# First attention of a two-layer decoder: the order of three engines, the sums of queries, and who normalizes

## The chip, the cores and the metric

The kernel runs on one core of a Trainium2 chip. A core has five engines that run side by side and meet only through semaphores: TensorE (PE, matrix products and transposes, result in PSUM), VectorE (DVE), ScalarE (ACT), GpSimd (POOL, which cannot read PSUM) and SyncE (SP, which here only issues DMAs). The metric is device microseconds of one execution; the median of several runs is compared.

## The reference, cut to what matters

A batch of 16 sequences of 112 tokens with 256 features passes through two decoder layers (attention, cross attention, mixture of experts, each behind a layer norm and with a residual). The change is in the first attention, a linear attention with 16 heads of 16 features:

```python
q = jax.nn.softmax(to_heads(q), axis=-1); k = jax.nn.softmax(to_heads(k), axis=-1)
comp_q = 1.0 - q; comp_k = 1.0 - k
def feat(x): return jnp.concatenate([x * sin, x * cos], axis=-1)
def branch(qf_, kf_):
    kv = jnp.einsum('bhld,bhlm->bhdm', kf_, v)
    z = 1.0 / jnp.maximum(jnp.einsum('bhld,bhd->bhl', qf_, kf_.sum(axis=2)), EPS)
    return jnp.einsum('bhld,bhdm,bhl->bhlm', qf_, kv, z)
attn = branch(qf, kf) + branch(comp_qf, comp_kf)
```

`sin` and `cos` depend on the token alone. The softmax of a query is its exponentials over their sum; the kernel works with the exponentials and puts the sums in at the end.

## The kernel before, in words

The whole program is one function, unrolled. A planner orders the instructions of each engine by a simulation of its own; inside `tc.manual_schedule(engines=...)` the engines named run their instructions in the order of the code. Before, the first attention names PE alone, so DVE, POOL, ACT and SP follow the planner. Each engine executes its queue strictly in order: an instruction that waits holds up all that stand behind it.

x stays in SBUF for the whole kernel (`x_res`). Its first two batches are loaded on SP, then Wq, Wk and Wv, then two more batches, then three groups of four, then Wo. ACT's queue loads the early constants, the output biases `bo2` of two attentions and the projection biases.

The stage is a software pipeline over the batches. Iteration i of its loop (L497) calls, for different batches:

- `norm0(i+2)` (L376): statistics on DVE (L232, L233), variance to a reciprocal root on POOL (L240, L241), normalization on DVE (L236), and the output bias added to x on POOL (L383).
- `norm0_T(i+1)` (L386): two transposes on PE, a copy on ACT (L390).
- `project0(i)` (L392): q, k and v products on PE (their matmuls all carry L115), biases added on DVE (L399, L403), the maximum of each head (L401), its subtraction on POOL (L404), exponentials on ACT (L405).
- `features(i-1)` (L408): q times sine and cosine on ACT (L415), transposes (L420), copy (L422); on DVE the sums of the exponentials of q and k (L425), reciprocals of the latter (L427), times sine and cosine (`rs`, L429); v scaled by them, one half on DVE and one on POOL (L433), with `rs` as eight more columns (L431); the products k by v on PE (L442), masked to the blocks of the heads on DVE (L449).
- `branches(i-2)` (L454): q by the masked product (L115, L458) and a constant product of the values for the complement (L459); the two normalizers z on DVE (L464 to L467), their combinations `sh` (L469, L470), two products into `a` (L472, L478), added on POOL (L484).
- `out_T0(i-3)` (L487): two transposes of `a` (L491), copied on ACT (L492).

In PE's order out_T0(i-3) stands ahead of features(i-1) and branches(i-2). After iteration 8 the vectors of later stages are transposed (`turn_vectors`) and an empty tile is written on POOL and spread to DRAM (`empty_rows`, L343). After the loop 16 output projections are added to x on DVE (L522); the second attention follows, whose own block names PE alone.

Of the kernel before, what the change touches and what calls it, by code (L numbers as in the profile page):

```python
# [33 lines left out]
def _constants():  # L34
# [9 lines left out]
    comp[:L] = both  # L44
    total = np.zeros((128, 1))
    total[:L, 0] = both.sum(axis=0)
    half = np.arange(8)
# [8 lines left out]
        "comp": comp,  # L56
        "total": total,
        "none_id": 2 * NT + p[:, None],
# [35 lines left out]
def tile_decoder(ctx: ExitStack, tc: tile.TileContext, t: dict, out: bass.AP):  # L94
# [38 lines left out]
    bo2 = cp.tile([L, 2, D], F32, tag="bo2", name="bo2")  # L133
    for i, n in enumerate(("L0_attn_bo", "L0_xattn_b_O")):
        nc.scalar.dma_start(bo2[:, i, :], t[n].partition_broadcast(L))

# [30 lines left out]

    w_attn0 = load_w(2 * WR, [t[f"L0_attn_W{n}"] for n in "qkv"])
    load_x(2, 2)
    for g in range(1, 4):  # L170
        load_x(4 * g, 4)
    w_attn0 += load_w(2 * WR + 1536, [t["L0_attn_Wo"]])
    nc.sync.dma_start(call[:, early:], t["consts"][:, early:])


    bV = cp.tile([KC, D], F32, tag="bV", name="bV")
    nc.sync.dma_start(bV, t["L0_xattn_b_V"].partition_broadcast(KC))
# [185 lines left out]
    with ExitStack() as ph:  # L363
# [9 lines left out]
        heads = lambda a: a.rearrange("p (f h) -> p f h", f=2)  # L373
        qks, vas, tots, qfs, kvs, outs = {}, {}, {}, {}, {}, {}

        def norm0(b):  # L376
            mv = sm.tile([L, 2], F32, tag="nmv", name="nmv", bufs=4)
            r = sm.tile([L, 1], F32, tag="nr", name="nr", bufs=4)
            xn = lp.tile([L, D], F32, tag="xn", name="xn", bufs=3)
            stats_of(mv, x[:, b, :])  # L380
            rstd_pow(r, mv[:, 1:2])
            normed(xn, x[:, b, :], mv[:, 0:1], r)
            nc.gpsimd.tensor_add(x[:, b, :], x[:, b, :], bo2[:, 0, :])  # L383
            return xn

        def norm0_T(b, xn):  # L386
            pt = bank()
            for c in range(2):
                nc.tensor.transpose(pt[:, c * L : (c + 1) * L], xn[:, c * 128 : (c + 1) * 128], ident[:L, :L])
            nc.scalar.copy(xnT[:, :, b * L : (b + 1) * L], pt[:, : 2 * L].rearrange("p (c l) -> p c l", l=L))  # L390
# [16 lines left out]

        def features(b):  # L408
            qk, va = qks.pop(b), vas[b]
            q = qk[:, :16, :].rearrange("p h d -> p (h d)")  # L410
            k = qk[:, 16:, :].rearrange("p h d -> p (h d)")

            qs = lp.tile([L, 2, D], F32, tag="qs", name="qs")
            for s in range(2):
                nc.scalar.activation(qs[:, s, :], q, AF.Copy, scale=tok[:, s : s + 1])  # L415
            pq = bank()
            for f in range(2):
                for s in range(2):
                    o = (2 * f + s) * L
                    nc.tensor.transpose(pq[:, o : o + L], qs[:, s, f * 128 : (f + 1) * 128], ident[:L, :L])  # L420
            qf = lp.tile([128, 4, L], F32, tag="qf", name="qf")
            nc.scalar.copy(qf.rearrange("p n l -> p (n l)"), pq[:, : 4 * L])  # L422

            tot = sm.tile([L, 32], F32, tag="a0tot", name="tot", bufs=4)
            nc.vector.tensor_reduce(tot, qk, AX.X, ALU.add)  # L425
            rk = sm.tile([L, 16], F32, tag="a0rk", name="rk", bufs=2)
            nc.vector.reciprocal(rk, tot[:, 16:])  # L427
            rs = sm.tile([L, 2, 16], F32, tag="a0rs", name="rs", bufs=2)
            nc.vector.tensor_tensor(rs, bcast(tok, 16), over(rk, 2), ALU.mult)  # L429
            v2 = lp.tile([L, 2, 2, 136], F32, tag="v2", name="v2")  # L430
            nc.gpsimd.tensor_copy(v2[:, :, :, 128:], rs.rearrange("p s (f h) -> p f s h", f=2))  # L431
            for s, e in enumerate((nc.vector, nc.gpsimd)):
                e.tensor_tensor(  # L433
                    v2[:, :, s, :128].rearrange("p f (h m) -> p f h m", m=16),
                    va.rearrange("p (f h m) -> p f h m", f=2, m=16),
                    bcast(heads(rs[:, s, :]), 16),
                    ALU.mult,
                )
            kv = lp.tile([128, 2, 2, 136], F32, tag="kv", name="kv")
            for f in range(2):  # L440
                pk = bank()
                mm(  # L442
                    pk[:, :272],
                    k[:, f * 128 : (f + 1) * 128],
                    v2[:, f].rearrange("p s n -> p (s n)"),
                    start=True,
                    stop=True,
                )
                nc.vector.tensor_tensor(  # L449
                    kv[:, f], pk[:, :272].rearrange("p (s n) -> p s n", s=2), over(block, 2), ALU.mult  # L450
                )
            tots[b], qfs[b], kvs[b] = tot, qf, kv

        def branches(b):  # L454
            qf, kv, tot, va = qfs.pop(b), kvs.pop(b), tots.pop(b), vas.pop(b)
            po, pc = bank(), bank()
            for f in range(2):
                mm_sum(po[:L, f * 136 : (f + 1) * 136], [(qf[:, 2 * f + s, :], kv[:, f, s, :]) for s in range(2)])  # L458
            mm(pc[:L, :D], const("comp", L), va, start=True, stop=True)  # L459
            o3 = po[:L, :272].rearrange("p (f n) -> p f n", n=136)  # L460
            z = sm.tile([L, 2, 16], F32, tag="z", name="z")
            zs = [heads(z[:, i, :]) for i in range(2)]
            sq, zt = heads(tot[:, :16]), o3[:, :, 128:]
            nc.vector.scalar_tensor_tensor(zs[0], sq, EPS_Z, zt, ALU.mult, ALU.max)  # L464
            nc.vector.scalar_tensor_tensor(zs[1], sq, const("total", L), zt, ALU.mult, ALU.add)
            nc.vector.scalar_tensor_tensor(zs[1], sq, EPS_Z, zs[1], ALU.mult, ALU.max)
            nc.vector.reciprocal(z, z)  # L467
            sh = sm.tile([L, 2, 16], F32, tag="sh", name="sh")
            nc.vector.tensor_add(sh[:, 0, :], z[:, 0, :], z[:, 1, :])  # L469
            nc.vector.tensor_mul(sh[:, 1, :], tot[:, :16], z[:, 1, :])  # L470
            a = lp.tile([L, 2, D], F32, tag="a", name="a")
# [21 lines left out]

        with tc.manual_schedule(engines={mybir.EngineType.PE}):
            xns = {b: norm0(b) for b in range(2)}
            norm0_T(0, xns.pop(0))
            for i in range(B + 3):  # L497
                if i < B:
                    project0(i)
                if i + 2 < B:  # L500
                    xns[i + 2] = norm0(i + 2)
                if i + 1 < B:
                    norm0_T(i + 1, xns.pop(i + 1))
                if 0 <= i - 3:
                    out_T0(i - 3)
                if 0 <= i - 1 < B:
                    features(i - 1)
                if 0 <= i - 2 < B:
                    branches(i - 2)
                if i == 8:  # L510
# [960 lines left out]
```

## Time and profile before

| what | us |
|---|---|
| median of 4 runs | 1876.49 (1873.29 to 1878.6) |
| the profiled execution | 1870.06 |
| its span in the profile | 1868.3 |
| PE, DVE, ACT, POOL busy in the span | 1630.1, 969.2, 603.1, 520.6 |
| first projection product of the first attention starts | 16.70 |
| last projection of the first attention starts | 117.58 |
| its output projection starts | 140.55 |

A profile has one row for each instruction or group: line of the kernel, engine, operation, `out<-in` by the names of the tiles, partitions x elements, count, busy time and mean time of one, and the idle time of the engine just before, with what ended it. Windows give each engine's busy time in a stretch. Busy time of PE is of pipelined matmuls, so a busy PE need not be at its peak. A float32 matmul appears as two passes.

### The profile page before, as it was taken

The numbers are of one execution on the slowest core, as the hardware profiler recorded it, in microseconds if no ns is written. First come the engines' busy times: TensorE is split into PE (matmuls) and PEld (weight loads), VectorE is DVE, ScalarE is ACT, GpSimd is POOL, SyncE is SP. The second block draws the span as 40 slices with busy tenths as digits, with TensorE's granted clock in tenths as the row PEclk, the third lists the DMA queues.
The fourth block names the chain that finished last, engine by engine and source line by source line (L and its number), as shares of the span: only waits on it lengthen the run. The fifth ranks groups of instructions, "written<-read, shape, count | busy, mean of one in ns | idle before, by whom it ended". The sixth has DMA issues, their size and how long they took to land. (4 is left out here: it accounts for less than half of the span.)

```text
span 1868.3 us, 31175 instructions
## 1 busy us (share of the span) xinstructions
PE 1630.1 (87%) x11755; PEld 1225.0 (66%) x11755; DVE 969.2 (52%) x2637; ACT 603.1 (32%) x1440; POOL 520.6 (28%) x699
## 2 busy tenths in 40 slices
PE   5877888888992496999999899999998899989992
PEld 4765566666661374778787566666666788878882
DVE  6864566666653243877776544655455532222222
ACT  2430333333340252223323333434432233323330
POOL 5532111111103452333333344444443000030003
PEclk9997999999996698999999999999998899999996
DMA  9401111111102345100000100000001244454422
GB/s 266 139 1 41 41 40 41 42 42 38 40 23 82 111 145 193 50 1 1 1 1 1 40 10 17 18 17 17 17 9 46 74 145 145 152 172 165 158 85 65
DMA packets 93342, 125.60 MB, mean 67 GB/s; under 512 B 17761, under 2 KB 76298, under 8 KB 93194
## 3 DMA queue, kind: packets, MB, share of 16 engines
q1 hardware_dynamic: 85178, 107.88, 18.7%
q0 software_dynamic: 5184, 13.13, 2.3%
q10 hardware_dynamic: 2832, 2.60, 0.5%
q8 instruction: 95, 1.56, 0.4%
q14 instruction: 53, 0.43, 0.1%
HBM read 94.40 MB, written 21.18 MB: 62 GB/s over the span
## 5 line engine op out<-in xcount | busy, mean ns | idle before, releaser
L1193 POOL TENSOR_SCALAR pr<-pr,den 112x375 f32<-112x375 f32 x128 | 156.5, 1241 | 198.3 <-DVE den L1191 192.4
L1373 DVE SCALAR_TENSOR_TENSOR hT<-pT,vT,gt 128x264 f32<-128x264 f32 x128 | 62.9, 492 | 239.6 <-ACT gt L1372 239.4
L115 PE MATMUL pT<-xnT,w_all 128*128 128x224 f32 (+2 forms) x736 | 165.0, 376 | 6.2 <-DVE xnT L267 6.2
L115 PEld LDWEIGHTS pT<-xnT,w_all 128*128 128x128 f32 x736 | 133.8, 198 | 25.8 <-issue 14.6
L641 ACT ACTIVATE pr<-pT 125x336 f32<-125x336 f32 x256 | 94.6, 456 | 164.8 <-PE pT L632 164.8
L1410 POOL DMA_INDIRECT got<-eo,row x32 | 30.1, 941 | 387.2 <-PE pT L115 215.8
L115 PE MATMUL pT<-cT,w_all 128*128 128x375 f32 x384 | 136.8, 497 | 0.2 <-ACT cT L1142 0.2
L616 DVE TENSOR_REDUCE mx<-pT 112x1 f32<-112x375 f32 x256 | 125.7, 539 | 20.7 <-PE pT L614 20.2
L115 PE MATMUL pT<-w_all,cT 128*125 128x256 f32 (+1 forms) x384 | 135.2, 496 | 0.0
L115 PE MATMUL pT<-hT,w_all 128*128 128x264 f32 x512 | 119.6, 393 | 6.3 <-ACT hT L1378 6.3
L115 PE MATMUL pT<-w_all 128*128 128x264 f32 x512 | 119.4, 389 | 0.0
L115 PE MATMUL pT<-e1T,w_all 128*128 128x264 f32 x512 | 116.7, 386 | 0.0
L115 PEld LDWEIGHTS pT<-hT,w_all 128*128 128x128 f32 x512 | 99.1, 194 | 24.2 <-ACT hT L1378 6.7
L1090 POOL TENSOR_TENSOR pr<-pr,den 112x448 f32<-112x448 f32 x64 | 59.3, 948 | 199.1 <-DVE den L1088 142.2
L115 PEld LDWEIGHTS pT<-w_all 128*128 128x128 f32 x512 | 97.4, 192 | 16.4
L115 PEld LDWEIGHTS pT<-cT,w_all 128*128 128x128 f32 x384 | 72.8, 195 | 53.0 <-issue 13.7
L115 PEld LDWEIGHTS pT<-e1T,w_all 128*128 128x128 f32 x512 | 96.7, 190 | 16.1
L115 PE MATMUL pT<-w_all,oT 128*112 128x256 f32 x448 | 106.9, 385 | 0.0
L115 PE MATMUL pT<-w_all,xnT 128*112 128x256 f32 (+1 forms) x320 | 105.2, 477 | 0.9 <-ACT xnT L390 0.9
L115 PEld LDWEIGHTS pT<-w_all,cT 128*125 128x125 f32 x384 | 71.0, 191 | 45.1 <-issue 31.4
L1372 ACT ACTIVATE gt<-pT,vT 128x264 f32<-128x264 f32 x128 | 61.3, 480 | 110.7 <-PE pT L115 89.6
L1182 ACT ACTIVATE pr<-pT,top 112x375 f32<-112x375 f32 x128 | 72.4, 572 | 52.2 <-DVE top L1181 50.2
(247 smaller groups left out, 3018.1 us busy)
## 6 DMA issues: line engine op xcount, KB each, us to landing
w_all<-in_L_ffn_w_c_fc_dram SPq DMA_DIRECT2D x16, 1024.0 KB
w_all<-in_L_ffn_w_gate_dram SPq DMA_DIRECT2D x16, 1024.0 KB
w_all<-in_L_ffn_w_c_proj_dram SPq DMA_DIRECT2D x16, 1024.0 KB
cx<-in_ctx_dram SPq DMA_DIRECT2D x32, 375.0 KB
kz<-kn SPq DMA_DIRECT2D x256, 23.4 KB
xg<-fill SPq DMA_DIRECT2D x1, 5547.0 KB
xb<-xg SPq DMA_DIRECT2D x43, 129.0 KB
eo<-os SPq DMA_DIRECT2D x16, 264.0 KB
```

What stands on the lines that cost most here:

```text
L115: mm(o, l, r, start=(i == 0), stop=(i == len(terms) - 1))
L616: nc.vector.tensor_reduce(mx[b % 2][:, g, i, 16:17], ps[i][:L, :S], AX.X, ALU.max, negate=True)
L641: nc.scalar.activation(pr[:, i, :], pw[i][:KC, : NKC * L], AF.Exp)
L1090: nc.gpsimd.tensor_tensor(pr[:, k], pr[:, k], bcast(den[:, k, :], L), ALU.mult)
L1182: nc.scalar.activation(pr[:, i, :], ps[i][:L, :S], AF.Exp, bias=top[:, i : i + 1], scale=1.0, accum_out=den[:, i : i + 1],)
L1193: nc.gpsimd.tensor_scalar(pr[:, n, :], pr[:, n, :], den[:, n : n + 1], None, ALU.mult)
L1372: nc.scalar.activation(gt, ps[1][:, :HS], AF.Identity, bias=vec(n_v + e * NJ + j), scale=1.0)
L1373: nc.vector.scalar_tensor_tensor(hT[:, j, :], ps[0][:, :HS], vec(12 + e * NJ + j), gt, ALU.add, ALU.mult)
L1410: nc.gpsimd.indirect_dma_start(out=got[:, :], out_offset=None, in_=eo[b // HB][:, :], in_offset=bass.IndirectOffsetOnAxis(ap=row[k][:, b : ...
```

## The change

It does the following, all in the first attention or in the loads ahead of it:

1. PE, DVE and POOL run in the order of the code; the code of the loop is put in a new order. An iteration is now by_place(i-1), project0(i), norm0_T(i+1), features(i-1), norm0(i+2), branches(i-2), out_T0(i-3), stats0(i+3).
2. `norm0` is split: `stats0` makes the statistics and the reciprocal root one iteration earlier; the normalization itself goes from DVE to POOL.
3. `by_place`, new, takes the scaling of q, k and v out of `features`. The copy of `rs` into the eight columns goes from POOL to ACT.
4. The sums of the exponentials of q are no longer reduced on DVE. The tile kv gets eight more columns per half, which hold the block mask; it becomes two fixed tiles whose mask columns are written once. The product with q then yields, beside 136 columns, eight columns with the sum of q times sine plus the sum of q times cosine; ACT scales them by one over (sine + cosine) of the token into `sq`.
5. The clamp of the second normalizer (L466) is dropped.
6. Loads: x of batches 2 and 3 ahead of Wv and not behind it; the bias `L0_xattn_b_O` goes from ACT's queue to a later place in SP's.

```diff
-    w_attn0 = load_w(2 * WR, [t[f"L0_attn_W{n}"] for n in "qkv"])
+    w_attn0 = load_w(2 * WR, [t[f"L0_attn_W{n}"] for n in "qk"])
     load_x(2, 2)
+    w_attn0 += load_w(2 * WR + 1024, [t["L0_attn_Wv"]])
...
+    nc.sync.dma_start(bo2[:, 1, :], t["L0_xattn_b_O"].partition_broadcast(L))
...
+        kv2 = [l1.tile([128, 2, 2, 144], F32, tag=f"kv{i}", name=f"kv{i}") for i in range(2)]
+        for kv in kv2:
+            nc.vector.tensor_copy(
+                kv[:, :, :, 136:].rearrange("p f s h -> p (f s) h"), over(block[:, 128:], 4)
+            )
+
+        def stats0(b):
             mv = sm.tile([L, 2], F32, tag="nmv", name="nmv", bufs=4)
             r = sm.tile([L, 1], F32, tag="nr", name="nr", bufs=4)
             stats_of(mv, x[:, b, :])
             rstd_pow(r, mv[:, 1:2])
-            normed(xn, x[:, b, :], mv[:, 0:1], r)
+            mvs[b] = mv, r
+
+        def norm0(b):
+            mv, r = mvs.pop(b)
+            xns[b] = lp.tile([L, D], F32, tag="xn", name="xn", bufs=3)
+            nc.gpsimd.tensor_scalar(xns[b], x[:, b, :], mv[:, 0:1], r, ALU.subtract, ALU.mult)
             nc.gpsimd.tensor_add(x[:, b, :], x[:, b, :], bo2[:, 0, :])
...
+        def by_place(b):
+            qk, va = qks[b], vas[b]
             q = qk[:, :16, :].rearrange("p h d -> p (h d)")
             qs = lp.tile([L, 2, D], F32, tag="qs", name="qs")
             for s in range(2):
                 nc.scalar.activation(qs[:, s, :], q, AF.Copy, scale=tok[:, s : s + 1])
+
+            tot = sm.tile([L, 16], F32, tag="a0tot", name="tot", bufs=2)
+            nc.vector.tensor_reduce(tot, qk[:, 16:, :], AX.X, ALU.add)
+            nc.vector.reciprocal(tot, tot)
+            rs = sm.tile([L, 2, 16], F32, tag="a0rs", name="rs", bufs=2)
+            nc.vector.tensor_tensor(rs, bcast(tok, 16), over(tot, 2), ALU.mult)
+            v2 = lp.tile([L, 2, 2, 136], F32, tag="v2", name="v2")
+            nc.scalar.copy(v2[:, :, :, 128:], rs.rearrange("p s (f h) -> p f s h", f=2))
+            for s, e in enumerate((nc.vector, nc.gpsimd)):
+                e.tensor_tensor(
...
                 nc.vector.tensor_tensor(
-                    kv[:, f], pk[:, :272].rearrange("p (s n) -> p s n", s=2), over(block, 2), ALU.mult
-                )
-            tots[b], qfs[b], kvs[b] = tot, qf, kv
+                    kv[:, f, :, :136], pk[:, :272].rearrange("p (s n) -> p s n", s=2), over(block, 2), ALU.mult
+                )
+            qfs[b] = qf
...
-                mm_sum(po[:L, f * 136 : (f + 1) * 136], [(qf[:, 2 * f + s, :], kv[:, f, s, :]) for s in range(2)])
+                mm_sum(po[:L, f * 144 : (f + 1) * 144], [(qf[:, 2 * f + s, :], kv[:, f, s, :]) for s in range(2)])
...
-            sq, zt = heads(tot[:, :16]), o3[:, :, 128:]
+            sq = sm.tile([L, 2, 8], F32, tag="sq", name="sq")
+            zt = o3[:, :, 128:136]
+            nc.scalar.activation(sq, o3[:, :, 136:], AF.Copy, scale=sums[:, 1:2])
             nc.vector.scalar_tensor_tensor(zs[0], sq, EPS_Z, zt, ALU.mult, ALU.max)
-            nc.vector.scalar_tensor_tensor(zs[1], sq, const("total", L), zt, ALU.mult, ALU.add)
-            nc.vector.scalar_tensor_tensor(zs[1], sq, EPS_Z, zs[1], ALU.mult, ALU.max)
+            nc.vector.scalar_tensor_tensor(zs[1], sq, sums[:, 0:1], zt, ALU.mult, ALU.add)
             nc.vector.reciprocal(z, z)
...
-        with tc.manual_schedule(engines={mybir.EngineType.PE}):
-            xns = {b: norm0(b) for b in range(2)}
-            norm0_T(0, xns.pop(0))
+        with tc.manual_schedule(engines={mybir.EngineType.PE, mybir.EngineType.DVE, mybir.EngineType.Pool}):
+            for b in range(2):
+                stats0(b)
+                norm0(b)
+            norm0_T(0)
+            stats0(2)
             for i in range(B + 3):
+                if 0 <= i - 1 < B:
+                    by_place(i - 1)
                 if i < B:
                     project0(i)
+                if i + 1 < B:
+                    norm0_T(i + 1)
+                if 0 <= i - 1 < B:
+                    features(i - 1)
                 if i + 2 < B:
-                    xns[i + 2] = norm0(i + 2)
-                if i + 1 < B:
-                    norm0_T(i + 1, xns.pop(i + 1))
+                    norm0(i + 2)
+                if 0 <= i - 2 < B:
+                    branches(i - 2)
                 if 0 <= i - 3:
                     out_T0(i - 3)
-                if 0 <= i - 1 < B:
-                    features(i - 1)
-                if 0 <= i - 2 < B:
-                    branches(i - 2)
+                if i + 3 < B:
+                    stats0(i + 3)
```

## What I expect, on record before the run

> **What bounds the kernel now.** I read the page's slices first: TensorE (PE) is busy 87% of the 1868.3 us span, and the chain that ended last is PE work at the end of the kernel. That decides nothing for a change that lives in the first attention, so the stage's own windows come next. Columns: start and end, length, then busy us (count) of PE, weight load, VectorE (DVE), ScalarE (ACT), GpSimd (POOL), then granted clock, DMA share, GB/s.
>
> ```profile
> 0.00:20.00 20.00, 3.93 (x10) 2.75 (x11) 6.89 (x24) 1.63 (x2) 7.95 (x23) 1.00 0.93 238
> ...
> 100.00:121.00 21.00, 19.71 (x113) 16.16 (x112) 17.95 (x61) 8.40 (x18) 10.29 (x15) 1.00 0.00 1
> 121.00:140.00 19.00, 11.36 (x54) 8.91 (x52) 8.54 (x33) 4.09 (x9) 4.28 (x6) 0.82 0.00 0
> ```
>
> The stage has three parts. In the first 20 us PE hardly works; in the middle PE (94%) and DVE (85%) are both nearly full; in the tail PE works 11.4 of 19 us, partly at a lower clock. The timeline (start, us, engine, line, tiles) says what holds each part.
>
> ```profile
> 12.86 0.38 POOL L240 TENSOR_SCALAR nr<-nmv 112x1 f32<-112x1 f32 x2 [6.92 <-DVE nmv L233]
> ...
> 13.20 2.14 POOL L241 TENSOR_TENSOR nr<-nr,power 112x1 f32<-112x1 f32 x4
> ...
> 15.18 1.45 DVE L236 TENSOR_SCALAR xn<-x_res,nmv,nr 112x256 f32<-112x256 f32 x3
> ...
> 16.70 5.20 PE L115 MATMUL pT<-w_all,xnT 128*112 128x256 f32 x12 [0.43 <-ACT xnT L390]
> ```
>
> Start: the planner put L240 of batches 2 and 3 ahead of L241 of batch 0 on POOL. Their x lands at 11.9, so batch 0, whose x was there at 4.6 and whose L240 ran at 5.54, stands behind them until 13.20, and the first projection starts at 16.70.
>
> ```profile
> 86.81 2.75 PE L115 MATMUL pT<-w_all,xnT 128*112 128x256 f32 x12
> ...
> 92.50 2.75 PE L115 MATMUL pT<-w_all,xnT 128*112 128x256 f32 x12
> ...
> 96.20 0.41 PE L491 MATMUL pT<-call,a 112*128 112x112 f32 x2 [0.75 <-POOL a L484]
> ...
> 134.13 0.63 PE L491 MATMUL pT<-call,a 112*128 112x112 f32 x2 [2.43 <-POOL a L484]
> ```
>
> Middle: one iteration of PE without a wait takes 92.50 - 86.81 = 5.69 us; most take 6.1 to 6.6, because the output transposes (L491) stand ahead of the feature products and wait for POOL's add (L484). From the projection of batch 1 (22.53) to that of batch 15 (117.58) the mean is 95.05 / 14 = 6.79, one iteration near 75 with 10.1 (69.99 to 80.12; context statistics, a blocked DVE, half a clock) included. Tail: from 117.58 to the output projection at 140.55 are 22.97 us, with the same wait for L484 up to 3.05 us long.
>
> **Start.** In written order POOL does L240 and L241 of batch 0 at once: 5.5 + 0.22 + 0.08 + 0.57 = 6.4, then the normalization (priced below, 0.9), transposes and copy (0.7 + 0.35): 8.4. The weights can be later. By the bytes moved (1.79 MB up to 9.0 us), x of two batches, the early constants, both output biases, Wq, Wk and two projection biases (1.41 MB) land between 7.5 and 9; one bias leaves that queue. I take 9.2 for the first projection, 7.5 us before 16.70. At half clock, as before (5.20), it ends at 14.4, so batch 1 starts at 14.4 and not 22.53: **-8.1**. x of batches 2 and 3 goes ahead of Wv: their statistics then cannot block DVE, and Wv (landing about 11) is first needed at 9.2 + 3.5 = 12.7, so that edit costs nothing; without this cover it would cost Wv's lateness once, under 2 us.
>
> **Middle.** PE's work stays: eight passes of 144 and not 136 columns add 8 x 8 columns, 0.03 us. DVE loses the normalization (0.40 to 1.04, mean 0.52), half of the sums (L425 0.68; two reductions of the trace, 375 elements 0.54 and 512 elements 0.67, make 0.42 for 256) and one clamp (0.14). POOL loses the copy L431 (0.21 to 0.47), which goes to ACT, and gains the normalization. No row has a two-scalar operation of POOL on 112x256. From below, the two-input add of that shape takes 0.73; from above, two passes of a one-scalar operation, scaled between L240 (one element, 0.22) and L1193 (375 elements, 1.24), take 2 x 0.92 = 1.83. I take 0.92, one pass of that kind, being nearest in form. POOL then does 0.64 + 1.06 + 0.92 + 0.73 + 0.73 + 0.22 + 0.57 = 4.9 us an iteration.
>
> ```profile
> L1193 POOL TENSOR_SCALAR pr<-pr,den 112x375 f32<-112x375 f32 x128 | 156.5, 1241 | 198.3 <-DVE den L1191 192.4 <-DVE top L1181 6.0
> L383 POOL TENSOR_TENSOR x_res<-x_res,bo 112x256 f32<-112x256 f32 x16 | 11.7, 739 | 3.2 <-DVE xn L236 3.2
> ```
>
> No engine's sum is above 5.7, but three queues in written order close a loop. On POOL the scaled values of batch i-1 (v2's second half) stand behind the add of batch i-3 and the two small statistics operations; on PE the branches of i-2 stand behind the feature products, which need those values; on DVE the a tiles come out of these branches, and free POOL's add again. Link by link: DVE to POOL 0.14, add 0.73, L240 0.22 + 0.08, L241 0.57, v2 0.64, to PE 0.06, feature products 0.93, branch product 0.96, to ACT 0.20, the new scaled copy of the sums of queries 0.22 (ACT's 112x4 takes 0.205, its 128x112 0.287), to DVE 0.03, and from the first z to the second a 1.69 (131.30 to 133.20 in the tail, less the clamp step 0.21). With 0.04 between POOL's operations this is **6.5 us**. On top comes this:
>
> ```profile
> 34.45 1.06 POOL L404 TENSOR_TENSOR qk<-qk,top 112x512 f32<-112x512 f32 x1 [2.20 <-DVE top L401]
> ...
> 34.62 1.04 DVE L236 TENSOR_SCALAR xn<-x_res,nmv,nr 112x256 f32<-112x256 f32 x1
> ```
>
> A DVE operation of 0.40 that starts inside a POOL operation ends as that one ends. L433 on DVE (median 0.36) once took 1.26, L429 (0.13) once 0.94. Such meetings are rare now, since POOL works half of the time. After the change it works 70%, and rs and DVE's half of v2 fall in L241, with POOL's half waiting for DVE's. I add that half, 0.36 (bounds 0 and 0.9): **6.9 us**, so 14 x (6.9 - 6.79) = **+1.5**. The Trainium skill, "SBUF — State Buffer", section "Who interferes with whom", speaks against moving the normalization: a DVE operation with two SBUF inputs and a reading GpSimd operation exclude one another for the whole instruction. That agrees with these rows; by the rule in full, with all four such DVE operations of an iteration waiting for half a POOL operation, the loop would be above 7.5, and without it 6.5.
>
> **Tail.** The output transposes now stand behind the branches. The last feature products no longer wait for L484 of batch 14 (127.78, values ready at 125.8: -1.9), and the last branches not for the transposes of batch 14 (134.55 against 131.5: -3.0). The extra ACT step costs 0.45 twice: **-4.0**.
>
> **Clock and what follows.** In a loop of 6.9 PE is idle 1.2 us an iteration. A gap of 1.46 (67.06) left the clock at 1.00; 1.39 and 0.77 within two us halved it:
>
> ```profile
> 76.00:78.00 2.00, 2.00 (x8) 0.53 0.01 4
> ```
>
> That episode cost some 3 us. Before had one in the middle; I allow one more: **+3**. DVE's order now also covers the sixteen output adds (L522), between which the planner put the second attention's first statistics; if they follow, its start is up to 2.5 later (1.9 for statistics and normalization, 0.6 for a transposition): I take **+1**. The moved memset (0.31) and copy (0.19) of the empty rows delay POOL once; their 5.5 MB transfer has 80 to 156 us free of other traffic. Weights and x after that are unchanged.
>
> **Sum.** -8.1 + 1.5 - 4.0 + 3 + 1 = -6.6. The profiled execution took 1870.06 us (span 1868.3): 1863.5. It lay 6.4 below the median of the four runs, 1876.49; against that median I predict **1870**. About 0.2% (3.75 us) is what a measurement can tell from no change.
>
> **Rivals.**
> - Forecast, loop near 6.9: 1870, its own range 1864 to 1874; 0.45.
> - The port is hardly met and the clock holds: loop 6.5, 14 x -0.29 = -4; with -8 and -4 and neither allowance, 1860. For it: medians of L433 and L429 now show almost no meeting. Against: POOL is fuller; 0.20.
> - The gain is given back: weights land at 12 (+3), the second attention starts 2.5 later, so 1875. For it: in the first 20 us DMA is 93% busy; 0.13.
> - Slower: the PE gap grows past what the clock bears. Place: before the feature products. Each iteration at half clock adds 0.93 + 0.96 = 1.9 us, as both products lie in the loop. From four such iterations on the gain is gone (4 x 1.9 = 7.6); with seven, 1870 + 13 = 1883. A normalization of 1.83 would open that gap. For it: the halving at 76; against: 1.46 without one; 0.22.
>
> Faster: 0.20 and nine tenths of 0.45, 0.60. Same: 0.13 and the rest, 0.18. Slower 0.22. The range runs from the second case to the fourth: 1859 to 1883.
>
> **What would show it.** First projection near 9, its spacing in the middle near 6.9, POOL's normalization near 0.92, feature products waiting for v2 on POOL, no wait of L491 in the middle, 19 us from the last projection to the output projection. Wrong if spacing is under 6.4 (the loop is not closed) or over 7.4, or if granted clock falls to half between 30 and 110.

## The result, and the profile after

The changed kernel takes 1877.73 us (median of its runs, 1865.89 to 1887.35); the kernel before took 1877.03 beside it (1869.38 to 1883.02). The ratio is 1.0007, 95% interval 1.0000 to 1.0014: no change. The time lies in the range of the prediction, but its forecast of -0.35% did not come.

The profiled execution after took 1882.35 us (span 1880.6), 12.3 more than the one before. Only 2.6 of that lie in the changed code: the first scores of the second attention start at 181.19 in place of 178.59, 2.6 us later. From there to the end, in code that the change doesn't touch, before's execution took 1689.7, after's 1699.4, and those of eleven variants below 1693 to 1703. What sets that part was not followed. So the runs are compared by their medians, and the stages by landmarks in the first attention; P(i) is the first projection of batch i.

Three stretches of the first attention after, with the columns as before (busy us and count of PE, weight load, DVE, ACT, POOL; clock; DMA share; GB/s):

```profile
0.00:20.00 20.00, 10.34 (x24) 6.76 (x25) 5.45 (x17) 3.63 (x7) 10.97 (x21) 1.00 0.89 217
...
100.00:121.00 21.00, 17.98 (x104) 14.97 (x103) 17.39 (x53) 8.72 (x26) 13.55 (x18) 1.00 0.12 33
121.00:140.00 19.00, 13.48 (x62) 10.57 (x60) 11.69 (x41) 5.52 (x15) 5.53 (x7) 0.81 0.00 0
```

PE does 10.3 us of work in the first 20 where it did 3.9. In the middle it falls from 19.7 to 18.0 of 21: the loop predicted is there. The timeline of the start:

```profile
5.55 0.57 POOL L243 TENSOR_TENSOR nr<-nr,power 112x1 f32<-112x1 f32 x1
...
6.25 1.24 POOL L394 TENSOR_SCALAR xn<-x_res,nmv,nr 112x256 f32<-112x256 f32 x1
...
8.61 3.76 PE L116 MATMUL pT<-w_all,xnT 128*112 128x256 f32 x8 [0.43 <-ACT xnT L402]
...
13.62 2.05 PE L116 MATMUL pT<-w_all,xnT 128*112 128x256 f32 x4 [1.25 <-DMA w_all<-in_L_attn_Wv_dram]
...
16.48 4.65 PE L116 MATMUL pT<-w_all,xnT 128*112 128x256 f32 x12 [0.43 <-ACT xnT L402]
```

GpSimd takes batch 0 through without a detour and P(0) starts at 8.61, not 16.70. Then P(0) waits in its middle: Wv is late by 1.25 us, P(1) starts at 16.48, and it takes 4.65 us where e1 below has 2.84.

One iteration of the middle, cut to the links of the loop:

```profile
95.44 0.57 POOL L243 TENSOR_TENSOR nr<-nr,power 112x1 f32<-112x1 f32 x1
95.52 0.19 DVE L431 TENSOR_TENSOR rs<-call,tot 112x32 f32<-112x32 f32 x1
...
95.75 0.43 DVE L435 TENSOR_TENSOR v<-va,rs 112x256 f32<-112x256 f32 x1
...
95.97 0.68 POOL L435 TENSOR_TENSOR v<-va,rs 112x256 f32<-112x256 f32 x1
...
96.70 1.19 PE L456 MATMUL pT<-v,qk 112*128 112x272 f32 x4 [1.18 <-POOL v L435]
...
98.67 0.63 ACT L417 ACTIVATE qk<-qk 112x512 f32<-112x512 f32 x1 [2.27 <-POOL qk L416]
...
99.20 0.26 ACT L481 ACTIVATE sq<-pT,call 112x16 f32<-112x16 f32 x1
...
99.49 0.17 DVE L482 SCALAR_TENSOR_TENSOR z<-sq,pT 112x16 f32<-112x16 f32 x1 [0.97 <-ACT sq L481]
...
99.94 0.73 POOL L395 TENSOR_TENSOR x_res<-x_res,bo 112x256 f32<-112x256 f32 x1
...
100.23 0.47 DVE L486 TENSOR_TENSOR sh<-z 112x16 f32<-112x16 f32 x1
...
101.56 0.73 POOL L501 TENSOR_TENSOR a<-a 112x256 f32<-112x256 f32 x1 [0.90 <-DVE a L495]
```

From one L501 (94.43) to the next (101.56) are 7.13 us, with TensorE waiting 1.18 for v2. Two delays in it are not links of the prediction: L481 stands on ScalarE behind the exponential L417, which waits for GpSimd's L416; and L486 (0.17 us as L469 in before) takes 0.47 and ends at 100.70, when GpSimd's L395 ends (99.94 + 0.73 = 100.67).

And one iteration, from P(6) at 50.47 to P(7) at 64.52, is 14.05 us long:

```profile
53.25 0.43 DVE L234 BATCH_NORM_STATS2 st<-cx 125x6 f32<-125x256 f32 x1 [3.59 <-DMA cx<-in_ctx_dram]
...
56.57 0.43 DVE L234 BATCH_NORM_STATS2 st<-cx 125x6 f32<-125x256 f32 x1 [0.46 <-DMA cx<-in_ctx_dram]
...
59.39 2.18 PE L456 MATMUL pT<-v,qk 112*128 112x272 f32 x4 [5.59 <-POOL v L435]
...
61.37 2.13 PE L116 MATMUL pT<-kv,qf 128*112 128x144 f32 x8
```

These statistics are the second attention's. Their code is outside the written block, but the planner still places them between the block's instructions, and what is queued behind them may not pass: z, a, rs and v2 wait, then TensorE, 5.59 us, and it comes back at half speed (L456 took 1.19 in the iteration above). In before the same six started from 54.96 to 75.91, without a wait for the context; the first:

```profile
54.96 0.40 DVE L232 BATCH_NORM_STATS2 st<-cx 125x6 f32<-125x256 f32 x1
```

The tail:

```profile
125.91 0.63 ACT L417 ACTIVATE qk<-qk 112x512 f32<-112x512 f32 x1 [1.96 <-POOL qk L416]
...
128.35 0.41 DVE L428 TENSOR_REDUCE tot<-qk 112x16 f32<-112x256 f32 x1
...
130.34 2.18 PE L456 MATMUL pT<-v,qk 112*128 112x272 f32 x4 [1.96 <-POOL v L435]
132.31 2.13 PE L116 MATMUL pT<-kv,qf 128*112 128x144 f32 x8
```

From P(15) to the output projection are 21.03 us (22.97 before): the wait for L484 is replaced by one of 1.96 for v2, with half speed behind it. Before's tail had half speed too:

```profile
127.78 2.05 PE L442 MATMUL pT<-v,qk 112*128 112x272 f32 x4
```

### The profile page after: what moved, and what is told of

It reads as the page before. It is cut to its first block, busy times and chain, and to the rows that moved or that the text cites. A ratio compares the mean times of both kernels' runs of the same rounds, so it can differ in the third digit from the quotient of the medians.

```text
span 1880.6 us, 31180 instructions
## 1 busy us (share of the span) xinstructions
PE 1638.1 (87%) x11755; PEld 1230.0 (65%) x11755; DVE 965.8 (51%) x2607; ACT 606.7 (32%) x1472; POOL 535.5 (28%) x699
## 5 line engine op out<-in xcount | busy, mean ns | idle before, releaser
L116 PEld LDWEIGHTS pT<-hT,w_all 128*128 128x128 f32 x512 | 98.9, 193 | 23.9 <-issue 6.5
L242 POOL TENSOR_SCALAR nr<-nmv 112x1 f32<-112x1 f32 x96 | 21.6, 225 | 237.6 <-DVE nmv L235 236.3
```

The source lines that it names most:

```text
L116: mm(o, l, r, start=(i == 0), stop=(i == len(terms) - 1))
L242: nc.gpsimd.tensor_scalar(r, var, EPS_LN, None, ALU.add)
```

## The experiments

All are timed against the kernel before. Landmarks in us; "spacing" is the most frequent one of the middle iterations (before and e2 have no steady one: 5.69 to 7.33 and 6.04 to 8.20 beside the longest), "longest" the longest from P(2) on, "scores" the first scores of the second attention:

```
kernel              P(0)   P(1)  spacing longest P(15)  out proj scores  ratio (95%)
before             16.70  22.53   6.14    10.13  117.58  140.55  178.59  1
after               8.61  16.48   7.14    14.05  120.24  141.27  181.19  1.0007 (1.0000-1.0014)
e1 context later    8.88  14.78   7.15     7.52  111.78  133.09  173.15  0.9969 (0.9955-0.9984)
e2 planner         16.74  22.65   7.53     8.28  126.48  144.77  183.71  1.0056 (1.0039-1.0074)
e3 norm on DVE      8.10  15.25   6.85    15.20  116.19  135.87  174.93  1.0002 (0.9988-1.0016)
e4 branch first     8.44  14.97   6.38    14.75  110.99  126.39  165.43  0.9951 (0.9937-0.9964)
e5 = e1 + e4        8.90  14.62   6.38     6.75  101.93  117.33  154.68  0.9900 (0.9876-0.9924)
e6 = e5, Wv first   8.83  14.71   6.38     6.91  104.40  119.79  158.72  0.9918 (0.9891-0.9945)
e7 = e1, sh reduced 8.62  14.86   7.02     7.41  110.29  131.63  171.66  0.9974 (0.9953-0.9994)
e8 before, written  7.91  13.43  13.44    14.13  193.62  221.01  259.83  1.0458 (1.0429-1.0486)
e9 = e5, sh         8.83  14.08   6.12     6.76   99.49  115.94  156.03  0.9877 (0.9851-0.9904)
e10 = e1, q on DVE  8.49  14.89   6.53     7.05  105.58  124.39  164.47  0.9922 (0.9897-0.9948)
e11 = e1, v2 on DVE 8.32  14.13   7.55     7.94  115.92  137.35  174.72  1.0007 (0.9985-1.0029)
```

The theory: the change gains some 8 us at the start by the written order, and loses as much to that same order, at two places: the context's statistics (about 6 us) and a loop that it closes across four engines (0.3 to 1 us an iteration). The rivals: the granted clock, the load of GpSimd, or the transfers are the cause.

The landmarks are those of one execution for each kernel, and two differences in them lie outside the edited code. Wv lands at different times: eight of the variants have the first loads of after unchanged and VectorE and GpSimd in a written order (all but e2, e6 and e8), and their P(1) is at 14.1 to 15.3, not 16.48. And the sixteen output projections took 14.1 us at a granted clock of 1.00 in e5 and e11, 15.6 to 15.8 at 0.89 to 0.90 in before, e2, e3, e4 and e6, 16.6 to 16.8 at 0.84 in after, e1, e7, e9 and e10, 17.1 at 0.82 in e8; the scores move with that. The medians show mostly less than the landmarks: e5 is 23.9 us ahead of before at the scores, 17.2 in the median.

**e1, the context's statistics out of the written order.** (e5, e6, e7, e9, e10 and e11 have this edit too.)

```diff
-                nc.vector.tensor_add(x[:, b, :], x[:, b, :], po[:L, :D])
+                last_add = nc.vector.tensor_add(x[:, b, :], x[:, b, :], po[:L, :D]).ins
...
-                    stats_of(cmv[:, b * NKC + j, :], cx[:, j, :])
+                    with tc.issue_after(last_add):
+                        stats_of(cmv[:, b * NKC + j, :], cx[:, j, :])
```

> The changed kernel, but the statistics of the second attention's context (six L234 on cx, which stand among the first attention's VectorE instructions) are queued behind the last output addition of the first attention. Theory: the iteration of 14.05 us (projections at 50.47 and 64.52) is long because VectorE, now in written order, stands still for the context's transfer (3.59 us before one L234, 0.46 before another), TensorE is then left waiting 5.59 us for v2 and drops to half clock. Then no iteration is over 8 us, first to last projection goes from 111.6 us (8.61 to 120.24) to about 105, the output projection starts near 134.5 in place of 141.27, and the whole is 0.3 to 0.4% shorter than the changed kernel, so about 0.997 of the kernel before. Rival 1: the long iteration has another cause (the granted clock, or v2 late by itself); then a long iteration stays near 50 to 65 us and nothing is gained. Rival 2: the statistics only move; with some 3 us of VectorE work (six of 0.39 and six aggregates of 0.18) ahead of the second attention, its first scores come 3 us later after the output projection than the 39.9 us measured now, and the whole gains 0.2% or less.

The long iteration is gone, its place has 7.15 and 7.16 (47.74, 54.89, 62.05), and its half speed with it, so the clock was an effect. From P(1) to P(15) are 97.00 us and not 103.76. The output projection comes 8.2 earlier and the scores 8.0; but 2.7 of that stand at P(6) already (47.74 against 50.47), from a Wv that landed earlier, and from P(6) to P(15) the edit gains 5.7 (64.04 against 69.77). The moved statistics cost the second attention nothing (40.06 us between the two landmarks, 39.92 after). The theory holds; both rivals fall.

**e2, the planner orders VectorE and GpSimd again.**

```diff
-        with tc.manual_schedule(engines={mybir.EngineType.PE, mybir.EngineType.DVE, mybir.EngineType.Pool}):
+        with tc.manual_schedule(engines={mybir.EngineType.PE}):
             for b in range(2):
                 stats0(b)
```

> The changed kernel, but only TensorE is in written order; VectorE and GpSimd are ordered by the planner, as before the change. All other parts of the change stay. Theory: the written order of VectorE and GpSimd costs twice, the wait of L234 for the context's transfer and part of the longer spacing of projections (7.14 us against 5.7 to 6.6 in the kernel before). Then the spacing falls to 6.8 or less, the long iteration goes, and the whole is 0.998 or less of the kernel before. Rival: the spacing is that of a ring of data (v2 on GpSimd, feature products, branch, square sums, GpSimd's sum), which no order of VectorE takes apart while TensorE's order stays; the spacing stays at 7.0 to 7.3, and if the planner puts the context's statistics in the same place, the long iteration stays too: ratio 1.000 to 1.002.

```profile
11.89 0.37 POOL L242 TENSOR_SCALAR nr<-nmv 112x1 f32<-112x1 f32 x2 [5.90 <-DVE nmv L235]
...
12.23 2.14 POOL L243 TENSOR_TENSOR nr<-nr,power 112x1 f32<-112x1 f32 x4
```

In this timeline of e2 GpSimd's queue again has batches 2 and 3 ahead of batch 0, and P(0) is back at 16.74 with all other parts of the change in place. So the start is the order's. By the medians the written order is worth 0.5% (1.0056 against 1.0007), at the scores 2.5 us: a lead of 6.2 at P(15), the context's wait included, less 2.7 in the tail and 1.0 behind it. What the medians have beyond that lies behind the scores and was not followed. The theory of this run was half wrong: the long iteration goes, but the spacing does not fall. From P(2) to P(15) the mean is 7.19 us, 7.08 with the written order without the context's wait (e1), 6.71 in before. So what made the middle longer than before's is not the order of VectorE and GpSimd alone; the rival is nearer on that. The run keeps TensorE's new order beside the new work and doesn't separate the two (e4 does).

**e8, the written order on the kernel before.** The same words in before's own block, whose code has the features ahead of the branches and the statistics of a batch directly ahead of its normalization.

> The kernel before, with one edit: its first attention has VectorE and GpSimd in written order too, in the order that its code has (features of i-1 ahead of the branch of i-2, normalization on VectorE, sums of queries reduced on VectorE, old order of loads). Theory: the first projection is at 16.7 in the kernel before only because the planner puts statistics of later batches, whose x lands at 12 to 14 us, ahead of the first normalization on VectorE and of the first power on GpSimd; the written order alone brings it to 9 us or less, without GpSimd's normalization and without the new order of loads. The six statistics of the context then wait for its transfer as in the changed kernel, if they stand at the same place, so the whole lies within 0.997 to 1.003 of before. Rival: the first projection is bound by the transfers of x or of the weights; then it stays at 15 us or later.

```profile
111.59 2.18 PE L442 MATMUL pT<-v,qk 112*128 112x272 f32 x4 [4.60 <-POOL v L433]
```

P(0) at 7.91: the start comes from the order alone, without GpSimd's normalization or the new loads, as said. The size of the whole was missed: iterations of 13.4, TensorE waiting 4.6 us in each for v2 and running the products behind it at half speed. On VectorE this v2 is written behind the addition and maximum of the projection and behind the next batch's normalization, which waits for GpSimd's power, which stands behind GpSimd's subtraction; the features wait for v2, and the next projection for the features. Hardly anything overlaps. The moves of code in the change (by_place ahead of the projection, the statistics an iteration earlier) take these waits apart; that they are what makes a written order bearable was not run by itself.

**e3, normalization on VectorE** (L394 as `nc.vector.tensor_scalar`, same place).

> The changed kernel, but with the normalization of x (L394) on VectorE again, still in written order. Theory: GpSimd's 1.23 us for it is on the ring only through the 0.3 us for which L486 stands still beside GpSimd's addition behind it, since GpSimd had 5.3 us of six iterations left before L416 and as much before L501; VectorE gains 0.40 us of work (the duration of the same instruction before). The spacing moves by less than 0.4 us either way (6.8 to 7.4), and the long iteration stays: ratio to the kernel before within 0.998 to 1.003. Rival: GpSimd's order is the ring (sum, statistics, normalization, v2 in one queue); without 1.23 us in it the spacing falls below 6.5, 14 iterations give 9 us, and the ratio is near 0.996.

Spacing 6.85, 0.29 less, as expected by the theory; total not to be told from after. L486 is back at 0.17 us, since L395 runs earlier. The gain is about that meeting's 0.30, so GpSimd's 1.23 us are in the loop by the meeting, not by their length; VectorE's added 0.41 us could hide a part of it.

**e4, the branch ahead of the features.**

```diff
+                if 0 <= i - 2 < B:
+                    branches(i - 2)
                 if 0 <= i - 1 < B:
                     features(i - 1)
                 if i + 2 < B:
                     norm0(i + 2)
-                if 0 <= i - 2 < B:
-                    branches(i - 2)
                 if 0 <= i - 3:
```

> The changed kernel, but in each iteration the branch of batch i-2 is written ahead of the features of batch i-1 (and ahead of the normalization). Theory: the ring of 7.14 us goes a1 (L495), GpSimd's sum L501, eps and power, v2 on GpSimd, feature products L456, masks, branch products, square sums, z, a; the branch of a batch stands behind the feature products of the next, which stand behind GpSimd's v2, which stands behind GpSimd's sum of the branch before it. With the branch ahead, it no longer waits for the next batch's v2, and the spacing falls to what TensorE's and VectorE's own work leaves: TensorE was busy 18.0 of 21 us in the stretch from 100 to 121, so about 6.1 to 6.6 us. 14 iterations give 7 to 14 us less to the last projection, ratio 0.993 to 0.997 of the kernel before. Rival: VectorE's queue or GpSimd's v2 stays the last to come (the masks now wait for z and a of the branch ahead of them), and the spacing stays at 7.0 or over, ratio 1.000 or more.

6.38 us, and a tail of 15.4 and not 21.0, all of whose rows are at full speed: the scores come 15.8 us earlier than after. No engine's work changed, so the 7.14 were the loop and not the load of GpSimd, nor the work of the change. The 14.75 of the context's wait stay, as they should.

**e5, both.**

> The edits of e1 (context statistics behind the last output addition) and of e4 (branch of batch i-2 written ahead of the features of i-1) together. Theory: they are two separate losses and add up. e1 took the long iteration (14.05 us) away and kept the spacing of 7.15; e4 took the spacing to 6.38 and kept a long iteration of 14.75. Together no iteration is over 7.5 us, the spacing is 6.38, the output projection starts near 118 (126.4 in e4 less 8.3), and the whole is 0.991 of the kernel before (0.9951 less 0.004). Rival: with the branch ahead, the long iteration has a second cause (a half clock, or x and weights not landed), or the second attention must wait for its context or weights once it starts 8 us earlier than in e4; then the output projection is early, but the first scores, at 165.4 in e4, are no earlier than 163, and the ratio stays at 0.995.

The two losses add: 0.9900, scores 26.5 us earlier than after. TensorE now waits 0.3 us an iteration.

**e6, Wv ahead of x of batches 2 and 3 again.**

> As e5, and the weights of the values (Wv) are loaded ahead of x of batches 2 and 3 again, as before the change. Theory: the first projection waits for Wv (1.25 us before its last products in the changed kernel, 0.52 in e1) because x of two batches, 229 KB, goes ahead of it, and P(1) starts at 14.4 to 15 without that wait; but batch 2's statistics then start about 1 us later than now (12.37 in the changed kernel), and P(2) waits for them. The gain to P(3) is under 1 us, the ratio to the kernel before is the same as that of e5 within 0.1%. Rival: the first loads are the bound of the start; then P(2) and all later projections are 2 us earlier, ratio 0.1% below that of e5. Other rival: x late costs more than Wv late; then P(3) is later by 1 us or more than in e5.

P(0) to P(1) lasts no less (5.88, 5.72 in e5; there Wv was in time), but batch 2's statistics start at 13.12 and not 11.39, TensorE then waits 1.45 for v2 and runs the next projection in 4.15 in place of 2.76: P(3) at 28.09 against 25.39. The second rival holds: the new order of loads is worth 2.7 us in these two executions, not nothing; part of it can be the transfers' own spread, since x of batch 2 lands between 10.9 and 12.4 in the kernels that load it first. The total doesn't separate the two.

**e7 and e9, the standstill of VectorE.** e7, and in e9 the second move too:

```diff
-            nc.vector.tensor_add(sh[:, 0, :], z[:, 0, :], z[:, 1, :])
+            nc.vector.tensor_reduce(sh[:, 0, :], z.rearrange("p s h -> p h s"), AX.X, ALU.add)
-            nc.vector.tensor_mul(sh[:, 1, :], sq.rearrange("p f h -> p (f h)"), z[:, 1, :])
...
+            nc.vector.tensor_mul(sh[:, 1, :], sq.rearrange("p f h -> p (f h)"), z[:, 1, :])
             nc.vector.tensor_tensor(
                 a[:, 1, :].rearrange("p (h m) -> p h m", m=16),
```

> As e1, but the sum of the two reciprocals (L486, which takes two operands of SBUF) is a reduction over one operand, same numbers, same place. In the changed kernel L486 takes 0.468 us in the mean, 0.17 alone, and ends when GpSimd's addition of the bias (L395) beside it ends; in e4 it takes 0.77 and ends when GpSimd's subtraction L416 ends. Theory: VectorE with two SBUF operands stands still while GpSimd works, for the whole of GpSimd's instruction; with one operand it doesn't, the line takes 0.15 to 0.25 us, and the spacing falls by 0.2 to 0.4 us, from 7.15 to about 6.85: 4 us to the last projection, ratio 0.994 to 0.996. Rival: VectorE is slowed by something else at this place (its own pipeline, ScalarE); then the reduction takes 0.4 us or more too and the spacing stays at 7.15.

```profile
90.36 0.73 POOL L395 TENSOR_TENSOR x_res<-x_res,bo 112x256 f32<-112x256 f32 x1
...
90.64 0.19 DVE L486 TENSOR_REDUCE sh<-z 112x16 f32<-112x32 f32 x1
90.74 0.37 DVE L487 TENSOR_TENSOR sh<-sq,z 112x16 f32<-112x16 f32 x1
```

In e7's timeline the reduction runs through beside L395 in 0.19 us, and the next line with two SBUF operands takes over the wait: it ends at 91.11, L395 at 91.09. So the mechanism is the theory's, but only 0.13 us an iteration of the expected 0.2 to 0.4 came out, and the total is e1's. e9 moves that line too:

> As e5, with L486 as the reduction of e7, and the multiplication behind it (L487, two operands of SBUF as well) moved behind the first product with the branch (L489). In e4 and e5 VectorE is busy without a gap through the iteration of 6.38, L486 among it with 0.73 to 0.78 us against 0.17 alone, and TensorE idles only 0.3 us of an iteration, for GpSimd's v2. Theory: without the 0.6 us VectorE has a, and GpSimd its sum, normalization and v2, early enough; TensorE's own 6.07 us is what is left: spacing 6.05 to 6.15, 4 us to the last projection, ratio 0.987 to 0.989 of the kernel before. Rival: the standstill goes to the next line with two SBUF operands, as in e7, where L487 took 0.37 in place of 0.16 and 0.13 of 0.3 us was gained; then the spacing is 6.25 to 6.38 and the ratio that of e5, 0.990.

```profile
86.35 1.06 POOL L416 TENSOR_TENSOR qk<-qk,top 112x512 f32<-112x512 f32 x1
...
86.67 0.19 DVE L486 TENSOR_REDUCE sh<-z 112x16 f32<-112x32 f32 x1
```

L486 took 0.77 at this place in e4 and e5; now 0.19 in the middle of L416. Spacing 6.12, with TensorE busy 11.93 of 12.24 us in two iterations (81.54 to 93.78). At 0.9877 it has the lowest ratio, but its interval overlaps that of e5, and it is behind e5 at the scores (156.03 against 154.68): its tail is 16.5 us and not 15.4, its output projections ran at the lower clock. That it is better than e5 is not shown.

**e10, the sums of queries on VectorE again.**

```diff
-            tot = sm.tile([L, 16], F32, tag="a0tot", name="tot", bufs=2)
-            nc.vector.tensor_reduce(tot, qk[:, 16:, :], AX.X, ALU.add)
+            tot = sm.tile([L, 32], F32, tag="a0tot", name="tot", bufs=4)
+            nc.vector.tensor_reduce(tot, qk, AX.X, ALU.add)
...
-            nc.scalar.activation(sq, o3[:, :, 136:], AF.Copy, scale=sums[:, 1:2])
```

> As e1, but the sums of the queries come from VectorE's reduction over 32 heads again, kept for the branch, and ScalarE's square sums (L481) go. (The extra columns of the products stay and are not read.) In the ring of 7.14 us z (L482) idles 0.97 for L481, which stands behind the exponential (L417) on ScalarE, which waits for GpSimd's subtraction. Theory: z follows the branch products directly, about 0.5 us earlier; the reduction is 0.29 us longer (0.68 against 0.39), most of which GpSimd's v2 does not wait for (its rs is done 0.25 us ahead of it). Spacing 6.6 to 6.8, 14 iterations give 5 to 8 us, ratio 0.993 to 0.994 of the kernel before. Rival: L486 stands still until GpSimd is through with the bias addition L395 in any case; then z earlier gains nothing, spacing 6.95 to 7.3, ratio 0.997 as in e1.

```profile
92.38 0.63 ACT L417 ACTIVATE qk<-qk 112x512 f32<-112x512 f32 x1 [1.96 <-POOL qk L416]
...
92.63 0.17 DVE L482 SCALAR_TENSOR_TENSOR z<-tot,pT 112x16 f32<-112x16 f32 x1 [0.39 <-PE pT L116]
...
93.36 0.18 DVE L486 TENSOR_TENSOR sh<-z 112x16 f32<-112x16 f32 x1
```

In e10's timeline z follows the products while the exponential still runs, and L486 slips in before L395 starts. Spacing 6.53, 0.62 less than e1, and 0.9922 against 0.9969. Within this order taking the sums from the products is the dearest of the parts that were tried singly: it saves VectorE 0.29 us and puts ScalarE's queue on the path. Whether that pays with the branch ahead was not run.

**e11, v2 by VectorE alone** (both halves `nc.vector`).

> As e1, but both halves of v2 are made by VectorE. The profile names GpSimd's v2 as what TensorE waits for, 1.0 to 1.2 us in each iteration. Theory: GpSimd is only the last name in the ring; its v2 ends 0.06 us after VectorE could end both halves (GpSimd's at 94.09 in e7, VectorE's first at 93.60 plus another 0.43), and the 0.42 us more on VectorE hold up the addition, the maximum and with them GpSimd's subtraction and ScalarE's exponential and square sums: spacing 7.1 to 7.6, ratio 0.997 to 1.000. Rival: GpSimd's queue is the ring; freed of 0.69 us the spacing falls to 6.5 to 6.8, ratio 0.993 to 0.995.

Spacing 7.55, 0.40 longer than e1. The profile had named GpSimd's v2 as what TensorE waits for; with that work gone from GpSimd, TensorE waits 1.61 us for VectorE's. The name in the wait is the last link, and the loop is the cause.

## Why the prediction was off, step by step

The median lies in the range because the range was wide on both sides; the gain forecast did not come. At the first scores the sum was -6.6 (its own terms for the clock and the second attention included); the profile shows +2.6. The difference of 9.2 by its terms:

- **Start, P(0):** right in mechanism and size, 8.61 for 9.2. e2 and e8 show the cause, the order.
- **Start, P(1):** 16.48 for 14.4, +2.1. Failed step: "Wv (landing about 11)". It landed at about 13.6 in this execution and 13.0 in e1, so the cover of 12.7 was overrun. Also, the sum let P(1) follow P(0) at once; transposes and copy lie between (21.90 to 22.53 in before). P(0) 0.6 earlier than taken makes up for that. The 2.1 are this execution's: the eight variants with these loads have P(1) at 14.1 to 15.3, about what was predicted. The choice "that edit costs nothing" fails by e6 as well, towards gain: x of batches 2 and 3 ahead is worth 2.7 us there.
- **Middle:** 103.76 us from P(1) to P(15) for 96.6, +7.2. Without the context's statistics e1 measures 97.0. That this is so near is in part luck: its spacing is 7.15 for 6.9, and its first two iterations are shorter (4.96 and 6.44). Of the 7.2, 1.0 lies between P(1) and P(2), where P(1) ran slowly behind the wait for Wv, and 5.7 between P(6) and P(15). The 5.7 are the step that the prediction did not make: it named the context's statistics in the mean of before, but did not ask where they would stand in an order that nothing passes, and when their data land. The 10.1 us iteration of before, which went into the mean of 6.79, was no such case: there nothing waited for the context.
- **Middle, links:** the normalization takes 1.24, not the 0.92 taken, within the bounds. The shared access to SBUF costs about as much as was allowed (0.36), but at L486 (0.30), not where it was expected: rs and VectorE's half of v2 do fall in L243 (95.52 and 95.75, L243 until 96.01), and take 0.19 and 0.43; the queue of ScalarE (L481 behind L417, some 0.3) was not in the sum, which priced that step as if ScalarE were free. The rule of the Trainium skill ("SBUF — State Buffer", "Who interferes with whom") that spoke against the change is borne out for L486 beside L395 and L416. Its full price was an overestimate: one of the four operations was held up in an iteration, not all.
- **Tail:** 21.0 for 19.0, +2.0. Failed step: "values ready at 125.8", which is 8.2 behind P(15) in before, so that the last feature products could start 1.9 sooner. In the written order the exponentials of the last batch are done at 126.54, but VectorE takes their sums (L428) only at 128.35, behind the branch of batch 13; v2 is done and the products start 10.1 behind P(15), no sooner than in before (10.2). The half speed behind the wait costs some 2.4 us, but before's tail, from which the sum started, had it too. Of the -3.0, 1.7 came (the last branch starts 5.12 behind these products, 6.77 in before). In e2 the products start as late (10.0 behind P(15)), but run at full speed, and its tail is 18.3; with the branch first e4's is 15.4.
- **Second attention:** 39.92 for 39.04 from output projection to scores, +0.9; e1 has the same, so it isn't the context's statistics. The output projections took 16.61 us at a granted clock of 0.84, 15.75 at 0.89 in before: that is the 0.9. In e2, e3 and e4, with 15.65 to 15.75, the stretch is 38.9 to 39.1, as predicted.
- **Clock:** the +3 kept for one more episode is used up: the episodes are in the terms above (-3.0). One of the prediction's own signs of being wrong came: between 30 and 110 the granted clock fell to half (0.50 from 59.4 to 63.5), behind the context's wait.

Together 2.1 + 7.2 + 2.0 + 0.9 - 3.0 = 9.2. The outcome is nearest to the rival "the gain is given back", but the two reasons that this rival named, late weights (2.1, and 1.0 behind them) and the second attention (0.9), are the smaller part; the context's wait, 5.7, it did not name. The slower rival (half clock in each iteration) did not come: gaps of 1.18 us left the speed alone.

## What to carry to other kernels

When a queue gets a written order, list all that will stand in it, instructions of later stages that a planner still inserts too, and give each the time at which its data land: one that stands ahead of its data stops everything behind it. Then look for the loop: follow one batch from engine to engine until a link stands behind an earlier batch in some queue, and try the order of two blocks before any engine's load; e4 moved no work and came to 0.9951; e3 moved work and stayed at 1.0002, and e11 moved work and lost what e1 had gained. A column that spares one engine some work can put another engine's queue on the path (e10).

## What was not expected of the hardware

In e4's timeline:

```profile
61.67 1.23 POOL L394 TENSOR_SCALAR xn<-x_res,nmv,nr 112x256 f32<-112x256 f32 x1
62.20 0.19 DVE L431 TENSOR_TENSOR rs<-call,tot 112x32 f32<-112x32 f32 x1
...
65.11 1.06 POOL L416 TENSOR_TENSOR qk<-qk,top 112x512 f32<-112x512 f32 x1
65.42 0.78 DVE L486 TENSOR_TENSOR sh<-z 112x16 f32<-112x16 f32 x1
```

L486 stands still to the end of GpSimd's L416, which has two operands; L431, also with two operands in SBUF, runs in its usual 0.19 us in the middle of GpSimd's L394, which reads one tensor and two columns of scalars. The page's rule, as the prediction gave it, has every reading operation of GpSimd exclude such a line; these rows show it for L395 and L416 and not for L394, and the rows decide. Nor does the middle iteration above show it for L243, which has two operands of one element per partition: L431 runs inside it in 0.19 us. What tells the operations apart is not shown. And of the rows that the prediction found in agreement, that of L236 is no case of the rule as quoted, since L236 reads one tensor and two columns of scalars. It works the other way too: in e9 an L395 that starts just behind v2 on VectorE (90.07, 0.42 us) takes 0.98 and not 0.73.
